# A four-layer graph network on one core: batch 0's row factor from two powers, the identity by TensorE, two weights loaded first, and a tail with a third score buffer, planned backwards

## The chip, the cores and the metric

The kernel runs on one core of a Trainium2 chip. The metric is the device time of one execution in microseconds (us); the profile's span runs from the first to the last instruction. The engines are TensorE (PE; its weight loads are listed apart as PEld), VectorE (DVE), ScalarE (ACT), GpSimd (POOL) and SyncE (SP), which only issues transfers here.

## What is computed

32 batches of 512 tokens with 128 features pass four layers, each with a normalization and relu ahead and a residual sum after it. All share one 512 x 512 matrix `adj`.

```python
# layer 0: graph convolution
h = relu(layernorm(x));  A = adj + I;  d = sum(A, -1) ** -0.5
x = x + (d[:, None] * A * d[None, :]) @ h @ W.T + b
# layer 1: gated steps, five times, starting from h = relu(layernorm(x))
m = adj @ h; av = concat(m, m)
z = sigmoid(av @ w3.T + h @ u3.T);  r = sigmoid(av @ w4.T + h @ u3.T)      # biases left out here
hv = tanh(av @ w5.T + (r * h) @ u5.T);  h = (1 - z) * h + z * hv
# layers 2 and 3: attention over the edges of adj
h = relu(layernorm(x)) @ W;  e = leaky_relu(h @ a_src [:, None] + h @ a_dst [None, :]), masked by the edges
x = x + elu(softmax(e) @ h)        # layer 3: without elu
```

## The kernel before

The kernel does not write its instructions down in order. It describes operations with an engine, an estimated cost, a priority ("due") and the values they read and write, and a planner plays them against limited buffers and then emits them in the order found. `Val` is a value that takes a buffer of its kind when it is first written and gives it back after its last use. The planner tried 16 pairs of (last, hurry) and took the best end of its own model:

```python
    def run(self):
        for o in reversed(self.ops):
            o.tail = o.cost + o.delay + max((q.tail for q in o.then), default=0)
            o.first = o.waits
        uses = {v: v.uses for o in self.ops for v in o.vals}
        best = min(self.ends, key=lambda end: self.attempt(uses, *end))
        self.attempt(uses, *best)
        ...
    def attempt(self, uses, last, hurry):
        ...
            o.soon = min(o.due, last - o.tail * hurry)      # the priority on its engine
```

Buffers that matter below, among them "e", the 512 x 512 scores of one attention layer of one batch (at the start, `adj` lies in one):

```python
        "e": tiles(2, [P, C, N], "e"),
        "off": tiles(4, SMALL, "off"),
        "bank": tiles(8, TOKENS, "bank", psum),
```

The start: `adj` is loaded in four row blocks, turned on TensorE, copied by ACT, and its row sums are taken by ACT (two blocks) and DVE (two); their power -1/2 is made on POOL. Batch 0 is normalized on DVE, and then scaled by the degrees' power:

```python
    w0 = load("w0", [P, D], a["L0_gnn_W"], -994.5)
    ...
        raw[k] = load(k, [P, src.shape[1]], src, -993.3)       # k: w4, w3, w5, u3, u5
    ...
    def norm(b, y, due):                                        # batch 0 only
        xb = xs[b]
        mv, rstd = norm_stats(b, due)                           # rstd = (variance + eps) ** -0.5 on POOL
        for c in range(C):
            op("DVE", 0.16, due, ... y = (x - mean) * rstd ...)
    ...
            if b == 0:
                norm(b, y, -802)
                for c in range(C):
                    op("DVE", 0.16, -800, ... y = max(y, 0) * dinv ...)
            else:
                norm_relu(b, y, ...)
```

The first product, of batches 0 to 3, multiplies the rows with adj, whose diagonal blocks (`diag` = block + identity, made on DVE) are taken from another tile:

```python
                for lo, hi in ((0, c), (c, c + 1), (c + 1, C)):
                    if lo < hi:
                        right = diag.t[:, c, :] if lo == c else adjT.t[:, c, lo * P:hi * P]
                        nc.tensor.matmul(flat(p.t)[:, lo * P:hi * P], h.t[:, c, :], right, ...)
```

The attention of the last four batches (called near) keeps on the core what the others send through memory. It centers its rows on DVE and lets ACT apply the row factor later:

```python
    def center_relu(b, y, due):
        for c in range(C):
            op("DVE", 0.21, due, ... bn_stats(st[c], x[c]) ...)
            op("DVE", 0.07, due, ... bn_aggr(mv[c], st[c]) ...)
            op("DVE", 0.16, due, ... y[c] = max(x[c] - mean[c], 0) ...)
        ...                                                     # variance + eps, and its power on POOL
    def gat(b, l, due):                                         # near: b >= 28; l = 2, 3
        ...  # turn y on PE, copy on ACT (gT), heads on PE, exp on ACT (h_gat), g = exp * rstd on DVE ("off"), scale on ACT
        for j in range(C):
            op("DVE", 0.68, due + 3, ... e[j] = max(row, h[j]) * mask(j) ...)
        ...  # mix e with h on PE, divide by the sums on DVE, elu for layer 2, add to x, store for layer 3
```

In the profile of this kernel: L559 is the first product, L353 the turning of weights, L297 the copy of adj turned, L402 the powers, L423 and L596 the row arithmetic of batch 0, L431 to L433 the near centering (statistics, mean, centering), L743 the heads, L748 exp, L751 the row factor times exp, L756 the scaling, L785 the scores, L772 the spreading of a row, L794 (near) and L805 the mixing, L452 turns to features, L653 to L675 the gated step.

Of the kernel before, what the change touches and what calls it, by code (L numbers as in the profile page):

```python
# [15 lines left out]
P = 128  # L16
# [7 lines left out]
FAR0, FAR1 = 2, 4  # L24
RUN_UP = 8
# [14 lines left out]
class Op:  # L40
    def __init__(self, engine, cost, due, emit, delay):
        self.engine, self.cost, self.due, self.emit, self.delay = engine, cost, due, emit, delay
        self.waits, self.then, self.vals = 0, [], []


class Plan:
# [5 lines left out]
    def __init__(self, buffers, ends):  # L52
        self.buffers, self.ends, self.ops = buffers, ends, []

# [28 lines left out]

    def run(self):

        for o in reversed(self.ops):
            o.tail = o.cost + o.delay + max((q.tail for q in o.then), default=0)
            o.first = o.waits
        uses = {v: v.uses for o in self.ops for v in o.vals}
        best = min(self.ends, key=lambda end: self.attempt(uses, *end))  # L90
        self.attempt(uses, *best)
        assert self.end < math.inf, "the order has come to a stop"
        for o in self.order:
            o.emit()

    def attempt(self, uses, last, hurry):
        for v, n in uses.items():
            v.uses = n
            if v.kind:
                v.t = None  # L100
        for o in self.ops:
            o.waits = o.first

            o.soon = min(o.due, last - o.tail * hurry)
# [7 lines left out]
        now, count = 0.0, 0  # L112
# [6 lines left out]
        def start(e):  # L119
            if busy[e]:  # L120
                return
            kept = []
            while ready[e]:
                key = heapq.heappop(ready[e])
                o = self.ops[key[1]]
                opens = [v for v in o.vals if v.kind and v.t is None]
                short = [v for v in opens if len(free[v.kind]) < sum(u.kind == v.kind for u in opens)]
                if not short:
                    for v in opens:
                        v.t = free[v.kind].pop()  # L130
                    busy[e] = True
                    o.at = now
                    order.append(o)
                    post(now + o.cost, 0, o)
                    post(now + o.cost + o.delay, 1, o)
                    break
                kept.append(key)
            for key in kept:
                heapq.heappush(ready[e], key)

# [9 lines left out]
        while events:  # L150
            now, _, kind, o = heapq.heappop(events)
            if kind == 0:
                busy[o.engine] = False
                settle(o, True)
            else:
                done += 1
                settle(o, False)
                for v in o.vals:
                    v.uses -= 1
                    if not v.uses and v.kind:  # L160
                        free[v.kind].append(v.t)
            for e in ready:
                start(e)
# [5 lines left out]
def gnn_stack(ctx: ExitStack, tc: tile.TileContext, a: dict, out: bass.AP):  # L169
# [13 lines left out]
    def flat(t):  # L183
# [25 lines left out]
        "e": tiles(2, [P, C, N], "e"),  # L209
# [6 lines left out]
        "off": tiles(4, SMALL, "off"),  # L216
        "rden": tiles(3, SMALL, "rden"),
    }, [(last, hurry) for last in (170, 173, 176, 179) for hurry in (0.06, 0.08, 0.1, 0.12)])
# [15 lines left out]
    def load(name, shape, src, due, queue="SP", cost=0.45, delay=3.6):  # L234
        v = fixed(shape, name)
        q = {"SP": nc.sync, "POOL": nc.gpsimd, "AQ": nc.scalar}[queue]
        op(queue if queue != "AQ" else "ACT", cost, due, lambda: q.dma_start(v.t, src), w=[v], delay=delay)
        return v
# [17 lines left out]
    for b in range(B):  # L256
        v = Val("x", C)
        op("SP", 0.5, -1002 if b == 0 else max(-995 + b, STEPS * b - 20) if b >= 8 else -995 + b,
           lambda v=v, b=b: nc.sync.dma_start(v.t, x[b].rearrange("(c p) d -> p c d", p=P)), w=[v], delay=3.5 if b == 0 else 3 if b > 3 else 4)
        xs.append(v)  # L260
    adj_sb = Val("e", C)
    for c in range(C):
        e, q = (("ACT", nc.scalar), ("SP", nc.sync))[c % 2]
        op(e, 0.45, -1001, lambda c=c, q=q: q.dma_start(adj_sb.t[:, c, :], adj[c * P:(c + 1) * P, :]),
           w=[adj_sb[c]], delay=3 if c == 0 else 4.2)
    w0 = load("w0", [P, D], a["L0_gnn_W"], -994.5)
# [4 lines left out]
    for k in ("w4", "w3", "w5", "u3", "u5"):  # L271
        src = a[f"L1_gnn_{k}_w"]
        raw[k] = load(k, [P, src.shape[1]], src, -993.3)
# [15 lines left out]
    for c in range(C):  # L289
# [8 lines left out]
        if c < 2:  # L298
# [3 lines left out]
        else:  # L302
            op("DVE", 0.66, -801, lambda c=c: nc.vector.reduce_sum(deg.t[:, c:c + 1], adj_sb.t[:, c, :], axis=mybir.AxisListType.X),
               r=[adj_sb[c]], w=[deg[c]])
    op("DVE", 0.1, -801, lambda: nc.vector.tensor_scalar_add(deg.t, deg.t, 1.0), w=[deg])
    op("POOL", 1.0, -1000, lambda: nc.gpsimd.tensor_tensor(dinv.t, deg.t, mhalf.t, ALU.pow), r=[deg, mhalf], w=[dinv])

# [5 lines left out]
    for m in range(C):  # L313
        op("DVE", 0.16, -799.5, lambda m=m: nc.vector.tensor_add(diag.t[:, m, :], block(adjT.t, m), ident.t),
           r=[adjT[m], ident], w=[diag[m]])

    def right_factors(mT, due):


        made = fixed([P, 4, 2, 2 * P], "made", 4)  # L320
# [4 lines left out]
        f |= {k: (lambda i=i: made.t[:, i], made[i]) for i, k in enumerate((2, 1, 4, 6))}  # L325
# [20 lines left out]
    def transposed(due, *group, then=()):  # L346

        p = Val("bank", len(group))
        t = fixed([P, len(group), P], "wT")
        for i, (parts, _) in enumerate(group):  # L350
# [3 lines left out]
            op("PE", len(parts) * MM1, due, turns, r=[ident, minus, *then] + [q[0] for q in parts], w=[p[i]])  # L354
# [13 lines left out]
    w0T = transposed(-750, (one(w0), 1), then=turned)  # L368
    gates = transposed(-700, (halves("w4"), 1), (one(raw["u3"]), 1), (halves("w3") + halves("w4", minus), 1), (halves("w5"), 1), then=turned)
    u5T = transposed(-690, (one(raw["u5"]), 0.5), then=turned)  # L370
# [21 lines left out]
    def norm_stats(b, due):  # L392
        xb, st, mv, ve, rstd = xs[b], Val("st", C), Val("mv"), Val("ve"), Val("rstd")
# [8 lines left out]
        op("POOL", 1.0, due, lambda: nc.gpsimd.tensor_tensor(rstd.t, ve.t, mhalf.t, ALU.pow), r=[ve, mhalf], w=[rstd])  # L402
        return mv, rstd

    def norm_relu(b, y, due, times=None):

        xb, off = xs[b], Val("off")
        mv, rstd = norm_stats(b, due)
# [9 lines left out]
    def norm(b, y, due):  # L418

        xb = xs[b]  # L420
        mv, rstd = norm_stats(b, due)
        for c in range(C):
            op("DVE", 0.16, due, lambda c=c: nc.vector.tensor_scalar(  # L423
                y.t[:, c, :], xb.t[:, c, :], mv.t[:, c, 0:1], rstd.t[:, c:c + 1], op0=ALU.subtract, op1=ALU.mult),
               r=[xb[c], mv, rstd], w=[y[c]])

    def center_relu(b, y, due):

        xb, st, mv, ve, rstd = xs[b], Val("st", C), Val("mv", C), Val("ve"), Val("rstd")
        for c in range(C):  # L430
            op("DVE", 0.21, due, lambda c=c: nc.vector.bn_stats(st.t[:, c, :], xb.t[:, c, :]), r=[xb[c]], w=[st[c]])  # L431
            op("DVE", 0.07, due, lambda c=c: nc.vector.bn_aggr(mv.t[:, c, :], st.t[:, c, :]), r=[st[c]], w=[mv[c]])
            op("DVE", 0.16, due, lambda c=c: nc.vector.tensor_scalar(  # L433
                y.t[:, c, :], xb.t[:, c, :], mv.t[:, c, 0:1], 0.0, op0=ALU.subtract, op1=ALU.max),
               r=[xb[c], mv[c]], w=[y[c]])
# [115 lines left out]
    def product(h, due):  # L551

        p, m = Val("bank"), Val("m")
        for c in range(C):
            def times(c=c):
                for lo, hi in ((0, c), (c, c + 1), (c + 1, C)):
                    if lo < hi:
                        right = diag.t[:, c, :] if lo == c else adjT.t[:, c, lo * P:hi * P]
                        nc.tensor.matmul(flat(p.t)[:, lo * P:hi * P], h.t[:, c, :], right, start=c == lo == 0, stop=c == C - 1,  # L559
                                         skip_group_check=True)  # L560
            op("PE", MM, due, times, r=[h[c], adjT[c], diag[c]], w=[p, m])
# [3 lines left out]
    def normalized(begun):  # L565
# [18 lines left out]
        return anT, right_factors(anT, 0)  # L584
# [4 lines left out]
    def gcn(pair, due):  # L589
        first, ys = pair[0] < 4, []  # L590
        for i, b in enumerate(pair):
            y = Val("y", C) if first else Val("pair", 2)
            if b == 0:
                norm(b, y, -802)
                for c in range(C):
                    op("DVE", 0.16, -800, lambda c=c, y=y: nc.vector.tensor_scalar(  # L596
                        y.t[:, c, :], y.t[:, c, :], 0.0, dinv.t[:, c:c + 1], op0=ALU.max, op1=ALU.mult), r=[dinv], w=[y[c]])
            else:
                norm_relu(b, y, -798 if b == 1 else due + i, dinv if first else None)
# [4 lines left out]
        ms = [product(y, due + i) for i, y in enumerate(ys)] if first else products(*ys, factors["an"], due + 1)  # L604
# [301 lines left out]
```

## Time and profile before

| | |
|---|---|
| time, median of 3 (range) | 1633.63 us (1631.4 to 1633.82) |
| span of the profiled execution | 1631.2 us, 23929 instructions |
| POOL busy | 143.2 us (9%) |
| TensorE clock over the span | 0.999 |
| TensorE's longest single waits | 1.9 us (tail), 1.1 us (start), 0.8 us (start) |
| transfers | 157.72 MB, mean 97 GB/s |

A line of the profile names the program line, the engine, the operation, what is written from what, and times; "idle before" is what the engine waited just ahead of it, and for whom. A busy TensorE is not TensorE at its peak. One logical fp32 product shows as two instructions. The chain that ended last is followed back from the last instruction through whatever released each step.

### The profile page before, as it was taken

The numbers are of one execution on the slowest core, as the hardware profiler recorded it, in microseconds if no ns is written. First come the engines' busy times: TensorE is split into PE (matmuls) and PEld (weight loads), VectorE is DVE, ScalarE is ACT, GpSimd is POOL, SyncE is SP. The second block draws the span as 40 slices with busy tenths as digits, with TensorE's granted clock in tenths as the row PEclk, the third lists the DMA queues.
The fourth block names the chain that finished last, engine by engine and source line by source line (L and its number), as shares of the span: only waits on it lengthen the run. The fifth ranks groups of instructions, "written<-read, shape, count | busy, mean of one in ns | idle before, by whom it ended". The sixth has DMA issues, their size and how long they took to land.

```text
span 1631.2 us, 23929 instructions
## 1 busy us (share of the span) xinstructions
PE 1617.3 (99%) x7330; PEld 1169.2 (72%) x7330; DVE 1386.3 (85%) x3989; ACT 716.1 (44%) x1593; POOL 143.2 (9%) x136
## 2 busy tenths in 40 slices
PE   9999999999999999999999999999999999999998
PEld 7666666776776777777776766767677777676777
DVE  8968688898978898888898888888887888777888
ACT  5653443535335344444535345353443533434343
POOL 2200000010001100000111001110000000000001
PEclk9999999999999999999999999999999999999999
DMA  4134353534436344353433535344362323434010
GB/s 130 33 71 104 81 120 91 124 98 106 115 82 147 82 117 104 91 135 84 121 101 96 137 79 134 88 106 118 82 146 73 98 72 84 123 91 110 27 40 27
DMA packets 374176, 157.72 MB, mean 97 GB/s; under 512 B 201664, under 2 KB 355616, under 8 KB 374048
## 3 DMA queue, kind: packets, MB, share of 16 engines
q1 hardware_dynamic: 373760, 155.67, 38.5%
q8 instruction: 58, 0.95, 0.2%
q14 instruction: 70, 0.57, 0.1%
q10 hardware_dynamic: 288, 0.52, 0.1%
HBM read 86.25 MB, written 69.84 MB: 96 GB/s over the span
## 4 chain that ended last, share of the span: by engine, by line
PE 95%; DVE 3%; ACT 1%; DMA 0%; POOL 0%; issue 0%; DVEq 0%; POOLq 0%; ACTq 0%
PE bank L520 35%; PE bank L805 12%; PE bank L653 8%; PE bank L654 8%; PE bank L667 8%; PE bank L660 8%; PE bank L668 8%; PE bank L743 3%; PE bank L612 2%; PE bank L559 1%; PE bank L794 1%; DVE e L785 1%; PE bank L452 1%; POOL rstd L402 0%; DMA w<-in_L_gnn_w_w_dram 0%
## 5 line engine op out<-in xcount | busy, mean ns | idle before, releaser
L520 PE MATMUL bank<-made,S 128*128 128x256 f32 x1128 | 269.5, 380 | 1.2 <-ACT half L525 0.9
L402 POOL TENSOR_TENSOR rstd<-ve,mhalf 128x4 f32<-128x4 f32 x120 | 132.8, 1108 | 1397.5 <-DVE ve L400 1130.6
L520 PEld LDWEIGHTS bank<-made,S 128*128 128x128 f32 x1128 | 217.2, 196 | 40.4 <-issue 17.2
L525 ACT COPY half<-bank 128x256 f32<-128x256 f32 x282 | 104.4, 370 | 258.7 <-PE bank L520 255.7
L805 PEld LDWEIGHTS bank<-h_gat,e 128*128 128x128 f32 x1792 | 207.9, 192 | 13.0 <-issue 11.2
L805 PE MATMUL bank<-h_gat,e 128*128 128x129 f32 x1792 | 208.6, 275 | 0.0
L656 ACT ACTIVATE r<-bank,gate_bw 128x512 f32<-128x512 f32 x160 | 109.6, 685 | 213.5 <-PE bank L654 190.2
L672 DVE TENSOR_TENSOR hv<-hv,hT 128x512 f32<-128x512 f32 x160 | 109.3, 683 | 85.3 <-ACT hv L670 84.9
L658 DVE SCALAR_TENSOR_TENSOR rh<-r,hT 128x512 f32<-128x512 f32 x160 | 110.0, 687 | 67.4 <-ACT r L656 66.5
L653 PE MATMUL bank<-m,wT 128*128 128x512 f32 x320 | 163.7, 593 | 0.0
L667 PE MATMUL bank<-m,wT 128*128 128x512 f32 x320 | 163.4, 592 | 0.0
L654 PE MATMUL bank<-hT,wT 128*128 128x512 f32 x320 | 163.4, 592 | 0.0
L668 PE MATMUL bank<-rh,wT 128*128 128x512 f32 x320 | 163.4, 592 | 0.0
L660 PE MATMUL bank<-m,wT 128*128 128x512 f32 x320 | 163.3, 592 | 0.0
L670 ACT ACTIVATE hv<-bank,gate_bw 128x512 f32<-128x512 f32 x160 | 109.5, 684 | 118.9 <-PE bank L668 117.6
L785 DVE SCALAR_TENSOR_TENSOR e<-row,h_gat,maskT 128x512 f32<-128x512 f32 x224 | 161.4, 740 | 0.0
L520 PE MATMUL bank<-adjT,h 128*128 128x256 f32 x640 | 159.5, 380 | 0.5 <-ACT h L687 0.5
L520 PEld LDWEIGHTS bank<-adjT,h 128*128 128x128 f32 x640 | 123.3, 196 | 25.2 <-issue 13.4
L533 DVE TENSOR_TENSOR m<-half,bank 128x256 f32<-128x256 f32 x282 | 115.9, 412 | 24.3 <-ACT half L525 12.0
L662 ACT ACTIVATE z<-bank,gate_bw 128x512 f32<-128x512 f32 x160 | 109.6, 685 | 51.5 <-PE bank L660 49.8
L395 DVE BATCH_NORM_STATS2 st<-x 128x6 f32<-128x128 f32 x480 | 115.4, 279 | 4.7 <-DMA x<-in_x_dram 4.4
L654 PEld LDWEIGHTS bank<-hT,wT 128*128 128x128 f32 x320 | 60.8, 190 | 76.5 <-issue 75.1
(137 smaller groups left out, 2278.8 us busy)
## 6 DMA issues: line engine op xcount, KB each, us to landing
far<-sq SPq DMA_DIRECT2D x920, 64.0 KB
h<-far SPq DMA_DIRECT2D x240, 128.0 KB
gT<-far SPq DMA_DIRECT2D x56, 256.0 KB
row<-line SPq DMA_DIRECT2D x56, 256.0 KB
x<-in_x_dram SPq DMA_DIRECT2D x32, 256.0 KB
h<-far SPq DMA_DIRECT2D x28, 256.0 KB
out_dram<-x SPq DMA_DIRECT2D x28, 256.0 KB
hT<-far SPq DMA_DIRECT2D x104, 64.0 KB
```

Of the source, the lines that this page charges most:

```text
L395: op("DVE", 0.21, due, lambda c=c: nc.vector.bn_stats(st.t[:, c, :], xb.t[:, c, :]), r=[xb[c]], w=[st[c]])
L402: op("POOL", 1.0, due, lambda: nc.gpsimd.tensor_tensor(rstd.t, ve.t, mhalf.t, ALU.pow), r=[ve, mhalf], w=[rstd])
L520: nc.tensor.matmul(low(r), u[:, l, :], factors[k][0]()[:, l, :], start=fresh and l == 0, stop=l == 1, skip_group_check=not fresh)
L533: op("DVE", HV, due - 5, lambda: nc.vector.tensor_add(out(), u.t, low(t)), r=[u, t], w=[o])
L653: nc.tensor.matmul(flat(gate.t), gates.t[:, 0, :], flat(m.t), start=True, stop=False)
L654: nc.tensor.matmul(flat(gate.t), gates.t[:, 1, :], flat(hT.t), start=False, stop=True)
L658: op("DVE", V, due - 5, lambda: nc.vector.scalar_tensor_tensor(flat(rh.t), flat(r.t), 1.0, flat(hT.t), op0=ALU.add, op1=ALU.mult), r=[r, h ...
L660: op("PE", MM, due + 0.3, lambda: nc.tensor.matmul(flat(gate.t), gates.t[:, 2, :], flat(m.t), start=False, stop=True, skip_group_check=Tru ...
L667: nc.tensor.matmul(flat(cand.t), gates.t[:, 3, :], flat(m.t), start=True, stop=False)
L668: nc.tensor.matmul(flat(cand.t), u5T.t[:, 0, :], flat(rh.t), start=False, stop=True)
L785: op("DVE", 0.68, due + 3, lambda j=j: nc.vector.scalar_tensor_tensor(e.t[:, j, :], rows(row.t), h.t[:, j, D + 1:D + 2], mask(j), op0=ALU. ...
L805: nc.tensor.matmul(pt()[:, c, :D + 1], e.t[:, j, i * P:(i + 1) * P], h.t[:, j, :D + 1], start=(j == 0), stop=(j == C - 1))
```

## The change

It has four parts. (1) Batch 0's rows: instead of one power for the variance and one for the degree, with two passes of DVE over the rows, the two are multiplied first and one power gives the factor, for row blocks 0 to 2 and then for block 3; blocks 1 to 3 are then scaled by ACT with relu. (2) In batch 0's product the identity is added by TensorE, as one more product with `ident`, so that it does not wait for the diagonal tile. (3) w4 and w3 are loaded ahead of batch 1's x, and w0 behind it; the turning of w0, u3, w5 and u5 is put behind the first product in priority. (4) The tail: "e" gets a third buffer (until the last layer-0 product it holds factors that had a tile of their own), near centering goes to ACT with negated means from DVE, and the planner repeats its search: it lays the work out backwards from the end found, as late as it can go, and takes those times as priorities for the next attempt (from 1350 on in its own time). It can also put idle transposes on TensorE where it would rest in the tail.

```diff
-        "e": tiles(2, [P, C, N], "e"),
+        "e": tiles(3, [P, C, N], "e"),
-        "off": tiles(4, SMALL, "off"),
+        "off": tiles(6, SMALL, "off"),
-    }, [(last, hurry) for last in (170, 173, 176, 179) for hurry in (0.06, 0.08, 0.1, 0.12)])
+    }, [(179, 0.06), (175, 0.06), (177, 0.12)], 1350,
+        IDLE_FROM, lambda v: nc.tensor.transpose(v.t[:, 0, :], ident.t, ident.t))
...
-        best = min(self.ends, key=lambda end: self.attempt(uses, *end))
-        self.attempt(uses, *best)
+        for last, hurry in self.ends:
+            for again in range(6):
+                if again:
+                    late = self.put_off()
+                for o in self.ops:
+                    if not again:
+                        o.soon = min(o.due, last - o.tail * hurry)
+                    else:
+                        o.soon = late[o] / self.SLOT if o.at > self.near_end else o.due
+                self.attempt()
...
-        raw[k] = load(k, [P, src.shape[1]], src, -993.3)
+        raw[k] = load(k, [P, src.shape[1]], src, -994.5 if k in ("w4", "w3") else -993.3)
...
-        made = fixed([P, 4, 2, 2 * P], "made", 4)
+        made = Val("e", 4) if passing else fixed([P, C, N], "made", 4)
...
-    w0T = transposed(-750, (one(w0), 1), then=turned)
+    w0T = transposed(-9.2, (one(w0), 1), then=turned)
...
+    def norm_first(b, y):
+        xb, off, f = xs[b], Val("off", C), Val("rstd", C)
+        mv, ve = norm_stats(b, -802)
+        for parts in ((0, 2, 1), (3,)):
+            ...
+            def power(c=parts[-1], some=some):
+                nc.vector.reduce_sum(deg.t[:, c:c + 1], adj_sb.t[:, c, :], axis=mybir.AxisListType.X)
+                nc.vector.scalar_tensor_tensor(f.t[:, some], deg.t[:, some], 1.0, ve.t[:, some], op0=ALU.add, op1=ALU.mult)
+            op("POOL", 1.0, -802, ... f = f ** -0.5 ...)
+            op("DVE", 0.1, -801.5, ... off = -mean * f ...)
+        op("DVE", 0.2, -800.5, ... y[0] = max(x[0] - mean[0], 0) ...)
+        op("DVE", 0.2, -802, ... y[0] = y[0] * f[0] ...)
+        for c in range(1, C):
+            op("ACT", 0.385, -798, ... y[c] = relu(x[c] * f[c] + off[c]) ...)
...
     def center_relu(b, y, due):
-            op("DVE", 0.16, due, ... y[c] = max(x[c] - mean[c], 0) ...)
+                nc.vector.tensor_scalar_mul(off.t[:, both], mv.t[:, both, 0], -1.0)
+                op("ACT", 0.385, due, ... y[c] = relu(x[c] + off[c]) ...)
...
-                for lo, hi in ((0, c), (c, c + 1), (c + 1, C)):
+                if by_diag:
+                    terms = [(0, c, row[:, :c * P]), (c, c + 1, diag.t[:, c, :]), (c + 1, C, row[:, (c + 1) * P:])]
+                else:
+                    terms = [(0, C, row), (c, c + 1, ident.t)]          # batch 0
```

## The prediction

> **What bounds the kernel now.** I read the page's busy shares first, then the chain that ended last, then busy time by stretch, then what TensorE waited for, and last the start and the tail in order of time. Busy shares, clock by fortieths of the span, and the chain's shares:
>
> ```profile
> PE 1617.3 (99%) x7330; PEld 1169.2 (72%) x7330; DVE 1386.3 (85%) x3989; ACT 716.1 (44%) x1593; POOL 143.2 (9%) x136
> PEclk9999999999999999999999999999999999999999
> PE 95%; DVE 3%; ACT 1%; DMA 0%; POOL 0%; issue 0%; DVEq 0%; POOLq 0%; ACTq 0%
> ```
>
> TensorE is busy for 1617.3 of 1631.2 us and carries 95% of the chain. A change that removes no TensorE work can touch only the 13.9 us in which TensorE is not busy, and what a lowered clock costs. Where these 13.9 us lie is read from busy time by stretch (columns: PE, weight loads, DVE, ACT, POOL, clock, DMA share, GB/s):
>
> ```profile
> 0.00:20.00 20.00, 17.75 (x106) 15.56 (x107) 14.04 (x67) 10.18 (x24) 6.05 (x11) 1.00 0.80 220
> 20.00:60.00 40.00, 39.54 (x194) 30.92 (x193) 39.29 (x164) 24.64 (x60) 10.14 (x9) 1.00 0.22 49
> 100.00:1440.00 1340.00, 1338.09 (x5882) 957.51 (x5881) 1143.55 (x3173) 587.10 (x1278) 104.09 (x95) 1.00 0.42 104
> ...
> 1585.00:1615.00 30.00, 26.96 (x221) 25.12 (x220) 29.76 (x125) 13.88 (x51) 5.00 (x5) 0.98 0.04 10
> 1615.00:1626.80 11.80, 11.77 (x95) 11.57 (x93) 8.60 (x25) 1.88 (x9) 0.00 (x0) 0.90 0.16 46
> 1626.80:1631.20 4.40, 0.00 (x0) 0.00 (x0) 1.54 (x8) 0.00 (x0) 0.00 (x0) 0.99 0.42 119
> ```
>
> The ledger of TensorE's idle time: 2.25 us in the first 20, 0.46 until 60, 1.91 over the long middle, 1.81 from 1440 to 1550 (same view, three stretches left out here), 3.04 from 1585 to 1615, 4.40 after its last matmul. From 1585 to 1615 DVE is busy for 29.76 of 30 us, so there DVE sets the pace. Two lines of TensorE's waits in 1440 to 1632 say what it stood for, and the chain in that stretch runs almost wholly over DVE:
>
> ```profile
> PE bank L452 <- ACT h_gat L756: 1.9, 1, 1.9
> PE bank L794 <- DVE e L785: 1.0, 2, 0.6
> ```
> ```profile
> 1611.66 0.29 DVE mv L432 x3
> 1612.24 0.48 DVE y L433 x2
> 1612.79 0.20 DVE off L751 x3
> 1613.00 1.33 DVE e L785 x2
> ```
>
> The 1.9 us wait is for an ACT result, but ACT was itself held by the small DVE product (L751), which had stood behind statistics and centering (L431 to L433) of another unit. It also costs clock: the finer stretches show 0.91 in 1610 to 1615 and 0.75 in 1615 to 1620. On 2.96 and 5.00 us of busy time that is 0.27 + 1.25, about 1.5 us. So the tail lost 3.0 + 1.5 us to DVE.
>
> The start, in order of time:
>
> ```profile
> 8.79 1.16 PE L353 MATMUL bank<-ident,w 128*128 128x128 f32 x8 [0.84 <-DMA w<-in_L_gnn_w_w_dram]
> 10.54 0.88 DVE L596 TENSOR_SCALAR y<-y,dinv 128x128 f32<-128x128 f32 x4 [0.31 <-POOL dinv L306]
> 11.13 0.39 PE L559 MATMUL bank<-v,y 128*128 128x128 f32 x2
> ```
>
> TensorE stands for weights until 8.79, turns them, and begins batch 0's product at 11.1, just after the rows (10.54) that waited for the power of the degrees (POOL, 8.91 for 1.59).
>
> [...] 128x128 centering takes 277 ns, a 128x512 score 743, so moving many small instructions off DVE is worth more than their elements. [...] the same 128x4 power took 1.02 to 1.59 us in the first 20 us here[...].
>
> **The change, part by part.**
>
> *Start.* Batch 0's rows now take one factor, the power of (degree+1)(variance+eps), made in two POOL powers (rows 0 to 2, then 3), where one power of the variance and then one of the degrees stood. I trace it with the durations of the trace before. Statistics end at 6.35 as before; the first row sum on DVE (0.74 us) and ACT's second sum (at 7.13) give the power's input by 7.4; the power (1.0 to 1.6) ends at about 8.6 to 9.0. In the built order DVE then has one statistics instruction of batch 1 ahead of the scaling of row block 0. Batch 1's x is now issued behind w4 and w3 instead of w0. Queue bytes up to its end are 1792 KB, exactly what stood ahead of w4's end before, and w4 was there at 8.79. So: 8.8, then 0.25 and 0.22: block 0 at 9.4, product at 9.5, against 11.1. Blocks 1 to 3 come from ACT at about 0.4 each (9.9, 10.4, the last with the second power at 10.9), faster than TensorE takes them. w4 and w3 (1536 KB, by 7.9) are turned ahead of it. Adding the identity costs four more 128-column pieces: the four products take 512+128 columns instead of 512, 0.11 each, 0.44 in all; two instructions fewer. The product ends at 13.4, the five other turns (0.6) fill until 14.0, and batch 1's rows are there by then (statistics 11.1, power 12.4, ACT 12.9 to 13.3). Batch 1's product starts at 14.0 instead of 15.0: **gain 0.9 us**, the price of the identity included. DVE is full in 20 to 60 (39.29 of 40), so it must keep up: it sheds 1.1 + 0.9 us of batch 0's row arithmetic and takes on about 1.0 for new small ones; just enough.
>
> *Tail, DVE to ACT.* 32 centerings (0.215 us of busy time each, 4.3 for the 20 after 1580) leave DVE. 16 small negations come (about 0.13, as L751's 1.7 / 12). After 1580 that is 4.3 minus 10 x 0.13, **3.0 us off DVE**. ACT takes 20 more activations there at about 0.39 (L756's time), 7.9 us onto 17.7 in 52: a third of the time is still free.
>
> *Tail, third score buffer and planning backwards.* Scores of a third unit can be written while two are still read. In the built order one more score group (four instructions), two x updates and one last candidate's worth of mixing stand after the last gated step. Counting the rest with durations from this trace, DVE has 47.8 us after the last step (44.6 before) and TensorE 45.1 after the last candidate (40.9 before, by columns at 0.86 us per 512 and 0.11 per transpose). The steps thus end some 4 us earlier and more is left to overlap, but DVE still has a little more to do than TensorE. So I do not expect the tail's waits to vanish: of the 4.5 us lost, **3.0 back**. Of the 1.8 us between 1440 and 1550, **0.4 back**. The planner's new filler transposes do not occur in the built order at all, so they neither cost nor help.
>
> *Middle and end.* The order in the middle is rearranged (only about half of TensorE's sequence still lines up), with the same work. Its idle time is 1.9 us of 1340 and can move either way by about 1.5: 0. The end (two last divisions and adds, 1.5 us, then the store) keeps its form: 0.
>
> Sum: 0.9 + 3.0 + 0.4 = 4.3 us. Off the mean of the three runs (1632.95; their median, 1633.63, is near the top of 1631.4 to 1633.82), that is 1628.65; I say 1628.5.
>
> **Rivals.** (1) *DVE's relief lands on ACT.* Centering becomes a DVE to ACT to TensorE chain where it was DVE to TensorE, and near units already put exp, scaling and copies on ACT. For it: the 1.9 us wait came through ACT. Against it: ACT was busy 13.9 of 30 us. It would leave the tail as before: about 1632. (2) *The tail becomes TensorE-bound,* and all idle and clock loss from 1440 on returns: 4.5 + 1.8 + 0.9, time 1625.8. For it: 3.0 us off DVE equals the 3.0 us of idling. Against it: DVE's 47.8 us still exceed TensorE's 45.1 after the last step. (3) *The start's gain is given back:* DVE full until 60 us. Then 1629.5. (4) *The middle gets worse by reordering,* a few waits on ACT or on banks: up to 2 us more, 1630.5 to 1631.
>
> **Range and chances.** The bounds come from the rivals: 1623.5 if both the tail and the middle turn out well, 1633 if ACT eats the tail's gain. Two per cent is 33 us and the whole of TensorE's idle time is 13.9, so neither side of 2% is in reach: faster 0.005, within 0.99, slower 0.005.
>
> **What would show it.** TensorE's busy sum stays at 1616 to 1618, idle falls from 13.9 to about 10. Right at the start: batch 0's first product at about 9.5, batch 1's at 14.0. Right in the tail: idle in the last 45 us before the last matmul near 1.5 instead of 3.0, DVE's chain shorter, clock at 0.9 or better in every 5 us stretch. Wrong: a wait of 2 us or more on ACT's new activations, idle of over 3 us in the middle, or a first product later than 10.5.

## The result, and the profile after

| | before | after |
|---|---|---|
| time, median (range) | 1633.57 us (1631.4 to 1633.82, 6 runs) | 1623.68 us (1623.28 to 1624.05, 6 runs) |
| ratio to before | 1 | 0.9942, 95% interval 0.9929 to 0.9955 |
| span of the profiled execution | 1631.2 us | 1622.2 us |
| TensorE busy / not busy | 1617.3 / 13.9 us | 1614.2 / 7.9 us |

The change saves 9.9 us; 4.3 were predicted. Measured once more for experiment 8, the two stood 8.0 us apart (1631.88 and 1623.84): from one measurement to another the median of the kernel before moved by up to 1.7 us, that of the changed one by 0.2. The measured time is just inside the stated range, 0.2 us above its lower end. Busy shares, the clock by fortieths of the span, and the shares of the chain that ended last, of the kernel after:

```profile
PE 1614.2 (100%) x7326; PEld 1168.2 (72%) x7326; DVE 1378.4 (85%) x3971; ACT 725.3 (45%) x1628; POOL 146.4 (9%) x137
PEclk9999999999999999999999999999999999999999
PE 94%; DVE 3%; DMA 1%; ACT 0%; POOL 0%; issue 0%; SPq 0%; DVEq 0%; ACTq 0%; POOLq 0%
```

In the changed kernel L671 is the first product, L438 the turning of weights, L542 the near centering on ACT, L769 and L771 the gate z (product, activation), L777 and L779 the candidate hv (product, tanh), L784 the step's last update (hT), L894 the scores, L903 and L914 the mixing. Busy time by stretch of the kernel after (PE, weight loads, DVE, ACT, POOL, clock, DMA share, GB/s):

```profile
0.00:20.00 20.00, 18.59 (x102) 15.39 (x103) 14.26 (x72) 11.74 (x27) 7.33 (x13) 1.00 0.70 201
100.00:1440.00 1340.00, 1338.30 (x5872) 956.99 (x5871) 1139.24 (x3174) 584.26 (x1273) 107.61 (x96) 1.00 0.43 104
1500.00:1550.00 50.00, 50.00 (x233) 34.88 (x232) 39.98 (x109) 25.86 (x59) 4.74 (x4) 1.00 0.14 34
1585.00:1600.00 15.00, 15.00 (x135) 14.87 (x134) 14.79 (x51) 6.41 (x26) 1.01 (x1) 1.00 0.15 45
1600.00:1615.00 15.00, 14.42 (x127) 14.06 (x126) 14.64 (x52) 8.17 (x30) 2.02 (x2) 1.00 0.16 45
```

From 1440 to 1600 TensorE does not rest at all, and 0.6 us of gaps are left before its last matmul, with the clock full. DVE is as full as before (29.43 of 30 us from 1585 to 1615, against 29.76), but it no longer carries the chain that ended last: from the last gated step to the last matmul 28.9 us of that chain lay on DVE before, 5.6 us lie there now. Of TensorE's waits in the tail one is left, where there were five groups:

```profile
PE bank L903 <- DVE e L894: 0.5, 1, 0.5
```

**A sharper ledger.** "Not busy" understates what a wait costs. A matmul's record (its end is modelled by the profile) outlasts the time until the next may start: a 256-column one lasts 380 ns, and its successor starts 216 ns later when nothing is in the way. So a late successor leaves a gap of 0.46 us in the busy time while it is 0.62 late. I therefore took, for each record, the start of the next minus the undisturbed spacing of its size (0.111 us for 128 columns, 0.217 for 256, 0.431 for 512, close to the medians of the trace before: 0.112, 0.216, 0.429). The sums of these spacings are TensorE's work; the rest is lost time, the clock of 0.50 in the kernel before (1614.06 to 1617.48) included.

| us | work | 0-20 | 20-60 | 60-1440 | 1440-1550 | 1550 to the last matmul | after its start |
|---|---|---|---|---|---|---|---|
| before | 1611.5 | 4.4 | 1.1 | -1.5 | 3.0 | 6.9 | 4.7 |
| after | 1612.3 | 3.4 | 0.8 | -0.9 | -0.2 | 1.3 | 4.3 |

(In sum the spacings are about 0.1% long, which makes the long middle negative; only its differences mean anything. Adding the 1.05 us ahead of the first matmul gives the span.) The start lost 1.3 us less up to 60 us and got 0.8 us more work; the middle is 0.6 worse; **the stretch from 1440 to the last matmul lost 1.2 us instead of 10.0**. The gain is there. (The two traces are 9.0 us apart; the executions traced stand 0.6 us below and 0.3 us above the medians.)

### The profile page after: what moved, and what is told of

The parts are those of the page before. It is cut to its first block, busy times and chain, and to the rows that moved or that the text cites. A ratio compares the mean times of both kernels' runs of the same rounds, so it can differ in the third digit from the quotient of the medians.

```text
span 1622.2 us, 24004 instructions
## 1 busy us (share of the span) xinstructions
PE 1614.2 (100%) x7326; PEld 1168.2 (72%) x7326; DVE 1378.4 (85%) x3971; ACT 725.3 (45%) x1628; POOL 146.4 (9%) x137
## 4 chain that ended last, share of the span: by engine, by line
PE 94%; DVE 3%; DMA 1%; ACT 0%; POOL 0%; issue 0%; SPq 0%; DVEq 0%; ACTq 0%; POOLq 0%
PE bank L628 33%; PE bank L914 12%; PE bank L762 8%; PE bank L763 8%; PE bank L776 8%; PE bank L769 8%; PE bank L777 8%; PE bank L852 3%; PE bank L721 2%; PE bank L903 2%; PE bank L671 1%; PE bank L560 1%; DVE st L480 0%; POOL rstd L493 0%; DMA e<-in_adj_dram 0%
## 5 line engine op out<-in xcount | busy, mean ns | idle before, releaser
L628 PE MATMUL bank<-made,S 128*128 128x256 f32 x960 | 230.7, 380 | 0.5 <-DVE m L641 0.3
L914 PEld LDWEIGHTS bank<-h_gat,e 128*128 128x128 f32 x1792 | 210.6, 191 | 13.0 <-issue 10.5
L914 PE MATMUL bank<-h_gat,e 128*128 128x129 f32 x1792 | 212.4, 275 | 0.0
L628 PEld LDWEIGHTS bank<-made,S 128*128 128x128 f32 x960 | 184.2, 196 | 31.3 <-issue 12.3
L777 PE MATMUL bank<-rh,wT 128*128 128x512 f32 x320 | 163.4, 592 | 0.0
L779 ACT ACTIVATE hv<-bank,gate_bw 128x512 f32<-128x512 f32 x160 | 109.7, 686 | 119.5 <-PE bank L777 119.4
L769 PE MATMUL bank<-m,wT 128*128 128x512 f32 x320 | 163.1, 592 | 0.0
L894 DVE SCALAR_TENSOR_TENSOR e<-row,h_gat,maskT 128x512 f32<-128x512 f32 x224 | 160.7, 741 | 0.0
L771 ACT ACTIVATE z<-bank,gate_bw 128x512 f32<-128x512 f32 x160 | 109.5, 685 | 42.6 <-PE bank L769 39.9
```

The costliest lines, as they stand in the source:

```text
L628: nc.tensor.matmul(low(r), u[:, l, :], factors[k][0]()[:, l, :], start=fresh and l == 0, stop=l == 1, skip_group_check=not fresh)
L769: op("PE", MM, due + 0.3, lambda: nc.tensor.matmul(flat(gate.t), gates.t[:, 2, :], flat(m.t), start=False, stop=True, skip_group_check=Tru ...
L777: nc.tensor.matmul(flat(cand.t), u5T.t[:, 0, :], flat(rh.t), start=False, stop=True)
L894: op("DVE", 0.68, due + 3, lambda j=j: nc.vector.scalar_tensor_tensor(e.t[:, j, :], rows(row.t), h.t[:, j, D + 1:D + 2], mask(j), op0=ALU. ...
L914: nc.tensor.matmul(pt()[:, c, :D + 1], e.t[:, j, i * P:(i + 1) * P], h.t[:, j, :D + 1], start=(j == 0), stop=(j == C - 1))
```

## The experiments

Each was run with the kernel before beside it. Experiments 1, 2, 3 and 5 shared a chip (before: 1632.24 us), so did 4, 6, 7 and the first of 8 (1632.20), and the other four of 8 (1631.88). Lost time is from the ledger above, over the same stretches. Times from different chips can be compared to a microsecond or two at best, as the kernel before shows. And every edit makes the planner find another order for all that follows, so an experiment shows what an edit and its new order do together.

**1. Centering back on DVE** (planner, third buffer and start stay).

```diff
-                op("ACT", 0.385, due, ... y[c] = relu(x[c] + off[c]) ...)
...
+            op("DVE", 0.16, due, ... y[c] = max(x[c] - mean[c], 0) ...)
```

> The changed kernel with one thing undone: near centering is on DVE again (32 small instructions, no negations); third score buffer, backward planning and the new start stay. Theory R (relief: the tail was bound by DVE, moving centering off it is what counts): most of the tail's gain is lost, about 5 of 9.9 us, time 1628 to 1629. Theory P (planning: the tail's waits came from the order, not from DVE's load): loses 1 to 2 us, 1625. Theory B (buffer: scores of a third unit were what was missing): loses about 1, 1624.5.

Measured 1627.02 us (1626.92 to 1627.21), ratio 0.9967 (0.9954 to 0.9980): 3.3 us above the changed kernel. Of these 1.7 are 15 filler transposes that the planner now puts in (0.111 each); the lost time from 1550 on rises from 1.3 to 2.7.

**2. Two score buffers.**

```diff
-        "e": tiles(3, [P, C, N], "e"),
+        "e": tiles(2, [P, C, N], "e"),
...
-        return anT, right_factors(anT, 0, True)
+        return anT, right_factors(anT, 0)
```

> The changed kernel with two score buffers instead of three (the factors of the normalized matrix lie in a tile of their own again); ACT centering, backward planning and the new start stay. Theory B: loses 4 us or more, 1628 or above, with waits on scores in the last 40 us. Theories R and P: loses at most 1 us, 1624 to 1625.

Measured 1627.27 us (1626.89 to 1627.66), ratio 0.9968 (0.9955 to 0.9981): 3.6 us above the changed kernel, 1.0 of them fillers (9); lost time from 1550 on is 3.8. Relief and buffer weigh about the same when one is taken away, and neither accounts for most of the gain.

**3. Planned forward only.**

```diff
-            for again in range(6):
+            for again in range(1):
-    }, [(179, 0.06), (175, 0.06), (177, 0.12)], 1350,
+    }, [(last, hurry) for last in (170, 173, 176, 179) for hurry in (0.06, 0.08, 0.1, 0.12)], 1350,
```

> The changed kernel planned forward only, with the 16 pairs of before and no pass backwards; ACT centering, third buffer and the new start stay. Theory P: TensorE's idling between 1440 and 1550 (1.8 us before, 0 after) and most of that after 1585 come back, loses 5 to 7 us, 1629 to 1631. Theory R: loses the 3.2 us from 1440 to 1550 at most, and keeps the rest, 1626 to 1627. Theory B: loses under 2.

Measured 1635.89 us (1635.55 to 1638.2), ratio 1.0022 (1.0013 to 1.0030). With relief, third buffer and new start in place, but without the passes backwards, the kernel is slower than before. 59 fillers (6.5 us of TensorE time) stand in this plan; experiment 4 leaves them out.

**4. Forward only, without fillers.**

```diff
-        IDLE_FROM, lambda v: ...
+        math.inf, lambda v: ...          # no filler transposes
```

> The changed kernel planned forward only, as in the run c_forward (1635.9 us), but without the 59 filler transposes (0.11 us each, 6.5 us of TensorE time) that the forward plan put in there. If the fillers were what made that run slow: 1629 to 1631. If they only fill time in which TensorE would have rested: the same 1635 to 1636, with 6 us more loss in gaps. If they held the clock up, it is slower: 1637 and a stretch of half clock before the end.

Measured 1638.03 us (1636.6 to 1639.71), ratio 1.0037 (1.0024 to 1.0049). Fillers had helped: without them the work falls by 6.5 us, and the lost time from 1440 on rises from 6.7 to 14.2. Busy time by stretch, with fillers and then without; the clock is the number after POOL's:

```profile
1610.00:1620.00 10.00, 9.56 (x80) 8.69 (x79) 7.16 (x33) 7.32 (x29) 1.98 (x2) 1.00 0.01 2
```
```profile
1600.00:1610.00 10.00, 8.42 (x72) 7.78 (x70) 9.43 (x40) 5.40 (x18) 1.01 (x1) 1.00 0.10 29
1610.00:1620.00 10.00, 8.10 (x42) 6.17 (x41) 6.62 (x31) 6.88 (x27) 1.98 (x2) 0.83 0.00 0
```

0.83 over ten microseconds is 1.7 us lost, as much as 3.4 us would lose at the 0.50 that the kernel before shows from 1614.06 to 1617.48. In the wait next to it TensorE stood for the new centering on ACT (L542), and ACT had itself stood idle for the negated means from DVE (L539):

```profile
1612.51 1.86 ACT L542 ACTIVATE y<-x,off 128x128 f32<-128x128 f32 x6 [1.82 <-DVE off L539]
1612.96 1.21 PE L560 MATMUL bank<-ident,y 128*128 128x128 f32 x4 [1.90 <-ACT y L542]
```

So here it is DVE's order that holds up the chain from DVE over ACT to TensorE, not ACT's load. In the changed kernel itself the fillers have nothing to do: none is in its order.

**5. The new start alone, on the kernel before.**

```diff
 (kernel before)
+ norm_first: two-power row factor;  batch 0's product adds ident on PE
+ w4, w3 loaded ahead of x[1];  turning of w0, u3, w5, u5 put off
+ six "off" buffers;  new landing estimates for the loads in the planner
```

> The kernel before with the new start alone (row factor from two powers, identity by TensorE in batch 0's product, w4 and w3 first, turning of the other weights put off); planner, two score buffers and DVE centering as before. By the prediction 0.9 us faster than before, about 1632.6. By the ledger of the two traces (0.84 us less idle in the first 20 us, but 0.84 us more TensorE work for the identity) only 0.1 at 20 us and 0.4 at 60 us: 1633.1, not to be told from before. Batch 1's product starts at about 14.7 in either.

Measured 1638.22 us (1636.94 to 1639.04), ratio 1.0034 (1.0021 to 1.0047): slower by a third of a percent, which neither expectation had. Up to 1440 work and lost time together are 0.9 us less than before, in one trace each; from 1440 on it loses 15.2 us instead of 10.0. The forward planner found another tail, and this one is worse. Whether the edits of the first 20 us did that, or the two more "off" buffers, which the tail uses too, this run can't tell (see experiment 6).

**6. ACT centering alone, on the kernel before.**

> The kernel before with near centering on ACT alone; forward planning, two score buffers, old start. Theory R (DVE's load bounds the tail): 3 us of DVE work less in the last 50 us must show as about 3 us, 1629 to 1630. Theory P (the order decides, and each edit throws the forward planner's dice anew): no gain to be relied on; anywhere within 5 us of before, with TensorE's loss between 1440 and the end 8 to 15 us as in the forward-planned runs so far (10 before, 15 with the new start alone).

The edit is the inverse of experiment 1 on the kernel before, with six "off" buffers. Measured 1635.78 us (1634.79 to 1637.65), ratio 1.0021 (1.0013 to 1.0029). DVE's relief alone makes the kernel slower. Two stretches of this run and, below, of the kernel before:

```profile
1440.00:1550.00 110.00, 106.54 (x489) 75.02 (x488) 86.61 (x237) 44.20 (x102) 8.56 (x7) 1.00 0.30 76
1550.00:1618.00 68.00, 63.43 (x435) 53.13 (x434) 58.63 (x191) 37.07 (x119) 6.50 (x7) 1.00 0.08 22
```
```profile
1440.00:1550.00 110.00, 108.19 (x495) 76.37 (x494) 89.80 (x253) 44.26 (x98) 7.82 (x8) 1.00 0.31 80
1550.00:1618.00 68.00, 64.93 (x440) 55.16 (x439) 62.99 (x207) 29.05 (x90) 6.95 (x7) 0.97 0.10 28
```

DVE is less busy than before (58.63 of 68 us against 62.99), and TensorE rests more. Theory R, that relief of DVE is enough by itself, falls here. One thing was not separated: between 1440 and 1550 experiments 4, 5 and 6 lose the same 4.65 us (3.0 before), each with a wait of 1.8 us for DVE at about 1494 that the kernel before doesn't have, and the only edit that the three share is the six "off" buffers. So some 1.6 us of their loss may belong to these buffers under a forward plan; no run has them alone.

**7. The new planner alone, on the kernel before, without fillers.**

```diff
 (kernel before: DVE centering, two buffers, old start)
+ run() with put_off(): three pairs, five passes backwards each
```

> The kernel before with the new planner alone (three pairs, each with five passes backwards), its filler transposes switched off; DVE centering, two buffers, old start. Theory P: more than half of the 9.9 us, 1626 to 1628. Theory R or B: DVE's load and the buffers are unchanged, so at most the 3.2 us lost between 1440 and 1550, 1630 or above.

Measured 1629.77 us (1628.94 to 1630.5), ratio 0.9984 (0.9977 to 0.9991), 2.4 us below the kernel before. Lost time from 1440 to 1550 falls from 3.0 to 0.4, from 1550 on from 6.9 to 5.8. Faster by itself, the only one of the parts run alone that is, but less than I had expected of it: planning alone is not most of the gain either. (It keeps four "off" buffers.)

**8. The whole new tail on the old start, twice; the changed kernel once more; two edits of its start.**

```diff
 h_tail_only, h_tail_again: kernel before + planner + third buffer + ACT centering
 g_diag: changed kernel, batch 0's product by the diagonal tile again
-        ms = [product(y, due + i, pair[i] > 0) ...
+        ms = [product(y, due + i, True) ...          # and diag planned at -799.5
 i_old_loads: changed kernel, loads and turning of weights as before
```

> All of the tail (backward planning, third buffer, ACT centering) on the kernel before, with the old start: weights' turning, batch 0's rows and its product as before. If the new start brings 0.9 us, as predicted, 1624.6. By the ledger of the two traces, in which the new start is worth 0.1 to 0.4 us, 1623.8 to 1624.1, not to be told from the changed kernel.

> The changed kernel once more, to stand on the same chip beside the three runs on its start: 1623.3 to 1624.1.

> The changed kernel with one thing undone in the start: batch 0's product takes its diagonal blocks from the tile made on DVE again instead of adding the identity on TensorE. By columns the identity costs four logical products of 128 columns, two instructions of 0.11 us each: TensorE's work falls by 0.84 us. If the row factors, not the diagonal, are what the product waits for: 0.8 us faster than the changed kernel, with the first product at 9.3 as now. If the diagonal blocks on DVE (four of about 0.2 us) hold up the rows: first product at 9.8 or later and the time as the changed kernel's within 0.3.

> The changed kernel with the loads and the turning of weights as before (w0 first, then batch 1's x, w4 and w3 behind; all turned ahead of the first product); two-power factor and identity by TensorE stay. If early w4 and w3 are what lets the first product start at 9.3: it starts at 11 again, 0.9 us or more slower than the changed kernel. If turning is only moved (TensorE has to do it anyway, and batch 1's rows are ready by 14 in either case): within 0.4 us of the changed kernel.

> The kernel with the whole new tail and the old start once more (1623.3 us in another call), now on the same chip as the changed kernel. If the new start is worth the 0.9 us predicted, it is 0.9 slower than the changed kernel; if the identity's 0.84 us of work eat what the earlier start brings, within 0.3 of it.

| | us, median (range) | ratio to before (interval) | first product at | work |
|---|---|---|---|---|
| h_tail_only (other chip) | 1623.34 (1622.93-1623.95) | 0.9946 (0.9931-0.9961) | 11.4 | 1611.5 |
| after_again | 1623.84 (1622.76-1625.33) | 0.9951 (0.9938-0.9963) | 8.9 | 1612.3 |
| g_diag | 1624.60 (1623.49-1625.71) | 0.9953 (0.9941-0.9966) | 11.2 | 1611.5 |
| i_old_loads | 1624.26 (1623.73-1625.02) | 0.9952 (0.9939-0.9966) | 10.6 | 1612.3 |
| h_tail_again | 1623.21 (1623.02-1624.28) | 0.9947 (0.9934-0.9959) | 10.8 | 1611.5 |

The old start with the new tail is as quick as the changed kernel, within the spread. The new start is worth nothing that these runs can tell. In i_old_loads the first product stands behind the turning of weights again, at 10.6, and the time stays within 0.4 us: turning was only moved. In g_diag the first diagonal block, which waits for the copy of turned adj, stood ahead of the end of batch 0's statistics on DVE:

```profile
6.87 0.29 DVE L396 TENSOR_TENSOR v<-adjT,ident 128x128 f32<-128x128 f32 x1 [0.73 <-ACT adjT L385]
7.08 0.38 DVE L484 BATCH_NORM_AGGREGATE mv<-st 128x2 f32<-128x6 f32 x4
```

In that execution adj also landed about a microsecond later than in the changed kernel's (ACT's first sum began at 4.94 instead of 3.94), so its 11.2 us is not the diagonal's doing alone; and it lost 2.1 us from 20 to 60, against 0.8. Whether the identity by TensorE is cheaper or dearer than the tile is not settled.

## Why the prediction was right in direction and too small

The direction was right, and so was the place, the tail. That the time lies in the range is luck in part. Errors of opposite sign met: the tail gave 5.4 us more than its sum, the start nothing of its 0.9. And the lower end, 1623.5, is 0.8 below what the prediction names for it (1625.8 for rival 2, less 1.5 in the middle, is 1624.3); at 1624.3 the measured 1623.68 would have been outside.

**The tail** was put at 3.0 + 0.4 us; it gave 8.8 (10.0 lost before, 1.2 after). Two steps failed.

The first is the size of what could be won. I added up 3.0 + 1.5 us from 1585 on and 1.8 from 1440 to 1550, 6.3 in all, from "not busy" times and clock, and took the 13.9 us of rest as all that could be touched. By start-to-start spacing the same stretches lost 10.0. The half clock was sized about rightly (1.5; 3.4 us at 0.50 are 1.7). But 36 starts, late by 9.0 us in all, show as only 4.9 us of gaps; the other 4.1 lie under the end of the matmul record before (the constants' surplus takes 0.5 off the sum): the record is longer than the spacing, 380 ns to 216 for 256 columns.

The second is the sentence "DVE still has a little more to do than TensorE. So I do not expect the tail's waits to vanish." It rests on 47.8 us for DVE against 45.1 for TensorE behind the last gated step. In the trace after, from the end of the last candidate's product on, TensorE has 46.4 us of work by spacing (41.9 before), and DVE is busy for 46.3 us (44.5 before), 45.4 of them ahead of the last matmul. So DVE's sum was 1.5 us too large, TensorE's 1.3 too small, and there was no surplus on DVE. What TensorE lost behind that product fell from 6.7 us to 1.4. From there to the last matmul, before and after (columns as above):

```profile
1578.16:1626.77 48.61, 45.57 (x364) 42.53 (x363) 43.57 (x158) 18.66 (x64) 5.00 (x5) 0.96 0.06 17
1570.28:1618.13 47.85, 47.27 (x416) 46.47 (x414) 45.39 (x165) 23.41 (x83) 5.04 (x5) 1.00 0.13 39
```

A smaller slip: 7.9 us more on ACT's 17.7 in 52 leave half of its time free, not a third.

The step's end moved further than the "some 4 us" that I read from the count. The last candidate's product ends 7.9 us earlier, of which 4.5 are work that now stands behind it (4.2 by my count); the rest is loss that is gone ahead of it. And the last of the 160 updates of hT, the step's last DVE instruction, follows it in 3.4 us instead of 6.8, so it ends 11.3 us earlier. In order of time, before and after:

```profile
1577.14 1.02 PE L668 MATMUL bank<-rh,wT 128*128 128x512 f32 x2
1577.99 1.88 PE L660 MATMUL bank<-m,wT 128*128 128x512 f32 x4
1579.05 0.69 ACT L662 ACTIVATE z<-bank,gate_bw 128x512 f32<-128x512 f32 x1 [3.60 <-PE bank L660]
1581.24 0.72 ACT L670 ACTIVATE hv<-bank,gate_bw 128x512 f32<-128x512 f32 x1
1584.26 0.68 DVE L675 SCALAR_TENSOR_TENSOR hT<-hv,hT 128x512 f32<-128x512 f32 x1
```
```profile
1569.26 1.02 PE L777 MATMUL bank<-rh,wT 128*128 128x512 f32 x2
1570.32 0.69 ACT L779 ACTIVATE hv<-bank,gate_bw 128x512 f32<-128x512 f32 x1 [1.03 <-PE bank L777]
1572.97 0.68 DVE L784 SCALAR_TENSOR_TENSOR hT<-hv,hT 128x512 f32<-128x512 f32 x1
```

Before, the last candidate's product ends at 1578.16, but its tanh starts only at 1581.24: ACT had two gates z, the other batch's tanh and a copy ahead of it in its order, and TensorE made the products of z (L660) behind both candidates'. ACT stood idle for 3.60 us until the first of them was there. After, the product of z stands ahead of the candidate's, and the tanh follows in 0.04 us. These 3.1 us on ACT are most of the 3.4; DVE's part, from tanh to hT, went only from 3.0 to 2.6 us. In experiment 4 ACT's order and DVE's queue cost 1.4 us each. Until hT is there the last batch cannot enter its two attention layers, a chain in which each layer waits on DVE, ACT and TensorE in turn. The end of the last hT separates forward from backward plans:

| | last hT ends | from there to the last matmul | lost from 1440 on |
|---|---|---|---|
| forward: before, experiments 3, 4, 5, 6 | 1584.9 to 1588.0 | 41.6 to 44.6 | 6.7 to 15.2 |
| backward: planner alone (7) | 1577.2 | 46.7 | 6.2 |
| backward, without relief (1) | 1573.3 | 47.4 | 2.8 |
| backward, without third buffer (2) | 1571.3 | 50.1 | 3.6 |
| backward, both (after, 8's h_tail_only) | 1573.6 | 44.2 to 44.5 | 1.1 to 1.2 |

So planning backwards brings the last steps forward, and leaves more attention work behind them; with relief and the third buffer that work runs in 44 us. Without one of them it takes 47 to 50, of which fillers are 1.7 us in experiment 1 and 1.0 in 2, and in 2 another 2.7 us of work stand behind the step. The parts don't add up: the planner alone brings 2.4 us, relief alone (with six "off" buffers) -3.6, relief and buffer under a forward plan, with the new start, -5.8 (experiment 4), and all of them 8 to 10. What is shown is that the three together make the gain and that each is needed for all of it. That it works through the order of the last gated step is argued from this table; no run moved that step alone, and the lowest loss under a forward plan (6.7, with fillers) is close to the planner's alone (6.2). The third buffer alone was not run, nor the forward plan with the new planner's three pairs, so a part of experiment 4's loss may belong to the choice of pairs.

**Rival 2** (the tail becomes TensorE-bound) was the one that came true, and more fully than I had priced it. **Rival 1** did not in the changed kernel: ACT took the centerings at 390 ns each, and TensorE waited for none of them. Under the forward plan it did (0.8 us at most in experiment 3, 1.9 in 4), but in experiment 4 ACT was waiting for DVE then. **Rival 3** came true in its amount and not in its place: from 20 to 60 us the changed kernel lost 0.8 us, 1.1 before. **Rival 4** took about 0.6 us in the middle in the first two traces, within the 1.5 allowed. **The end** kept its form (4.7 and 4.3).

**The start** was put at 0.9. Its first half held: batch 0's product began at 9.30 (9.5 predicted). The second did not. In order of time, after:

```profile
9.30 1.02 PE L671 MATMUL bank<-adjT,y 128*128 128x512 f32 x2
13.41 0.38 PE L671 MATMUL bank<-ident,y 128*128 128x128 f32 x2
13.63 0.39 PE L438 MATMUL bank<-ident,u 128*128 128x128 f32 x2
14.74 0.39 PE L671 MATMUL bank<-v,y 128*128 128x128 f32 x2
```

Two terms were mis-sized, by the same slip. A logical fp32 product of 128 columns is two instructions of 0.11 us, not one. The identity therefore costs 0.84 us of TensorE work, not 0.44, and the five turns, which are plain products and not transposes, took 1.1 us (13.63 to 14.74), not 0.6. Batch 1's product began at 14.74, not 14.0. Batch 0's output product followed at 18.24, against 18.36 before; the changed kernel's second trace has 17.89. Against the old start with the same tail and on the same chip the whole part gives nothing measurable: in these two traces (after_again, h_tail_again) the new start loses 1.45 us less up to 60 us, but has 0.8 us more work and loses 1.1 us more between 60 and 1440. Why the middle loses more is open.

**The signs named.** TensorE's idle sum fell to 8 us rather than 10, its busy sum left the stated 1616 to 1618 downwards (1614.2), because busy time also holds what was lost before at half clock and under the ends of records. DVE's part of the chain is shorter and the clock full up to the last matmul, as stated for a right prediction. The signs of a wrong one stayed away: no wait on ACT's new activations, no 3 us of idling in the middle (1.7), first product before 10.5.

## What to carry to other kernels

When one engine is 99% busy, count lost time by the spacing of its starts, not by gaps between records; here that raised the tail's stake from 6.3 to 10.0 us. Before counting loads after some point, ask when that point comes: the last links of the last serial chain should not stand in an engine's order behind work whose inputs come later. Here the last tanh stood 3.1 us behind two gates, another tanh and a copy, and the plan laid out backwards had no such wait. A part that shows as useless alone, such as freeing an engine (3.6 us slower), can be worth 3 us once the order lets it be used; and a small edit can cost 5 us in the tail through a planner, so compare parts under the same planner and look where the time went.

## What was not expected of the hardware

The clock fell shortly after a wait, and stayed low for longer than the wait had lasted. In the kernel before TensorE waited 1.93 us, the matmul at 1613.57 started 2.1 us late by spacing, and from 1614.06 to 1617.48, for 3.4 us, the granted clock was 0.50:

```profile
1610.00:1615.00 5.00, 2.96 (x22) 2.49 (x21) 5.00 (x26) 2.91 (x11) 1.01 (x1) 0.91 0.00 0
1615.00:1620.00 5.00, 5.00 (x36) 5.00 (x35) 3.74 (x12) 1.18 (x7) 0.00 (x0) 0.75 0.18 52
```

At 0.50, 0.91 and 0.75 over five microseconds each make 0.9 + 2.5 = 3.4 us. In experiment 4 a wait of 1.90 us (2.1 late) lies in the stretch with 0.83. In experiment 5 the longest wait is 2.7 us (2.9 late), and the mean clock over its span is 0.999, as in the kernel before. A wait of 1.8 us at about 1494, in experiments 4 and 6, left the clock full (1.00 from 1440 to 1550). Ahead of the drop in the kernel before TensorE had not rested throughout: it was busy for 1.5 of the 3.4 us up to 1614.06. What tips the clock stays open. Experiment 3, planned the same way but with 59 filler transposes of 0.11 us, kept the full clock (1.00 from 1590 to 1630) and was 2.1 us quicker (1635.89 against 1638.03), though they are 6.5 us of work with no result. The first 20 us differ between executions of one start: eight traces with TensorE adding the identity lost 3.0 to 3.6 us there, five with the old start 4.1 to 5.2, so a start's gain under a microsecond cannot be read from one trace.
